# One-bank PSUM buffers for layer 1's transposes and last product, and no fetch of missing edges' rows in layer 2

## The chip, the cores and the metric

The kernel runs on one core of a Trainium2 chip. A core has four engines that compute and a set of DMA engines. TensorE (PE in the profile; PEld is its weight load) multiplies matrices and writes to PSUM, a memory of eight banks, each of which holds 512 float32 numbers in each of 128 partitions. VectorE (DVE) and ScalarE (ACT) work elementwise and read PSUM and SBUF. GpSimd (POOL) mostly issues gathers here, which are indirect DMAs with one row of a table for each partition. SyncE (SP) issues the plain DMAs. Each engine runs its own instructions in order and waits on semaphores for the others. The metric is the device time of one execution in microseconds, and the number given is a median over runs.

## What is computed

Two layers of graph attention over 10,000 nodes, each with a residual product, and a layer norm at the end. The edge list has 80,000 random edges in both directions and a self-loop for each node, 170,000 edges, sorted by destination. The reference adds the self-loops once more, so that each counts twice. Cut to what matters:

```python
def gat_conv(x, edge_index, W, a_src, a_dst, bias, heads, out_ch, concat):
    xl = (x @ W).reshape(n, heads, out_ch)
    alpha_src = jnp.einsum('nhc,hc->nh', xl, a_src)
    alpha_dst = jnp.einsum('nhc,hc->nh', xl, a_dst)
    e = leaky_relu(alpha_src[src] + alpha_dst[dst], 0.2)
    e = exp(e - segment_max(e, dst)[dst])
    alpha = e / (segment_sum(e, dst)[dst] + 1e-16)
    return segment_sum(xl[src] * alpha[:, :, None], dst) + bias

h = relu(layer_norm(gat_conv(x, ..., heads=4, out_ch=256, concat=True)))
h1 = h + (x @ Wr1 + br1)                                  # 10000 x 1024
h = layer_norm(gat_conv(h1, ..., heads=1, out_ch=768)) + (h1 @ Wr2 + br2)
out = layernorm(x + h)                                    # 10000 x 768, float32
```

## The kernel before

The work has three stages, and all three handle 79 tiles of 128 nodes.

**Preparation, with layer 1's first product (lines 602 to 670).** For each tile, x is multiplied by W1, and the product goes to `table1` in DRAM, with the logit terms of its four heads. A row has R1 = 1033 numbers: 1024 features, 4 + 4 logit terms, and minus the node's rank. Meanwhile the nodes are sorted by their number of edges, most first. Tile t in this order has `SLOTS[t]` edge slots for each node, a bound on the degrees that is known beforehand: 41 for the tile with the largest degrees, 8 for that with the smallest, 1377 in all. `slots` holds for each node and slot the row to be fetched. A node with fewer edges than its tile has slots has missing edges; their slot names row NP, one past the nodes' rows. That row is filled so that its logit is -1e30 and its weight zero.

**Layer 1 (`ordered_layer1`).** The tiles are taken in an order (`TURNS`) that runs from few slots up to 41 and down again. A ring of 29 row buffers in SBUF is filled by POOL, with one gather of 128 rows for each slot. `Ring.fetch` issues the gather of slot q + 29 when slot q has been used. The first 29 gathers read whatever their slot names. Later ones carry a bounds check at NP - 1, and a row past it is not fetched: the buffer keeps what it held. So that such a row has no weight, `logits` overwrites the logit columns of rows that it has read with -1e30 (line 489).

For each tile, DVE computes the logits, ACT their exp, and DVE the weights e. A few slots (`on_pe`, 1 to 4) are weighed on PE: ACT builds diagonal matrices of e, and PE multiplies the rows by them into the PSUM tile `acc`. ACT and DVE weigh the others (`multiply` at line 508, `weigh` at 515 and 519) and DVE adds them to `acc`. Then come the norm of the tile before (DVE, `h`), the transposes of x and h on PE, which ACT copies to SBUF (`columns`), x's product with Wr1 (`r`), and h's product with W2 (`to_layer2`), whose 770 columns ACT copies to `row` (`store`). They go to `table2`.

The order of the instructions is written by hand: the pools are under `manual_schedule`, and the loop over slots places the moves, the product for layer 2 and the next x's gather at given slots (`events`, `due`). PSUM is full: two `acc` tiles take four banks, `ps_h1` has one buffer of two banks for both transposes and the product for layer 2, and `ps_r1` has one of two banks for x's product.

**Layer 2 (`ordered_layer2`).** Again a ring, of 38 buffers with rows of R2 = 770 numbers from `table2`. A tile's first slot is its own nodes' rows, one contiguous block that SP loads (`ring.own`); POOL gathers the others, without a bounds check (line 453). `residual(t + 1)` multiplies h1 by Wr2 on PE, `weights_of(t + 1)` makes the weights and adds columns 512 to 767 of all slots on PE through diagonals (line 876), DVE weighs columns 0 to 511 (line 519), and `norms` finishes a tile over the next tile's slots and scatters it to the output (line 909).

Of the kernel before, what the change touches and what calls it, by code (L numbers as in the profile page):

```python
# [35 lines left out]
P = 128  # L36
# [43 lines left out]
def gnn_kernel(ctx, tc, x, x_cols, src, dst, src_col, dst_col, W1, a_src1, a_dst1, b1, g1, be1, Wr1, br1,  # L80
# [83 lines left out]
    def product(aT, w, n, pool=None):  # L164

        k = w.shape[1]
        p = (pool or ps_big).tile([P, 2 * BANK], F32, name="big")
        for c in range(0, n, BANK):
            e = min(n, c + BANK)
            for j in range(k):  # L170
                nc.tensor.matmul(p[:, c:e], aT[:, j, :], w[:, j, c:e], start=(j == 0), stop=(j == k - 1))  # L171
        return p
# [267 lines left out]
    class Ring:  # L440
# [8 lines left out]
        def fetch(self, upto):  # L449
            for q in range(self.issued, min(upto, TOTAL)):  # L450
                if q in self.own:
                    nc.sync.dma_start(self.slot(q), self.table[self.own[q] * P:(self.own[q] + 1) * P, :])
                elif q < self.size or self.own:
                    gather(self.slot(q), self.table[:, :], slots[:, q:q + 1])
                else:
                    gather(self.slot(q), self.table[:, :], slots[:, q:q + 1], bounds_check=NP - 1,
                           oob_is_err=False)
                self.issued = q + 1
# [12 lines left out]
    def logits(small, ring, lo, hi, ad, heads, c, top=None):  # L471


        n = hi - lo
        e = small.tile([P, ring.size, heads], F32, name="e")[:, :n]
        for a, b, rows in ring.parts(lo, hi):
            nc.vector.tensor_tensor(e[:, a - lo:b - lo], rows[:, :, c + heads:c + 2 * heads],
                                    ad[:, None, :].to_broadcast([P, b - a, heads]), op=OP.add)
        leaky(e, e)
        new = small.tile([P, heads], F32, name="new")  # L480
        nc.vector.reduce_max(new, e.rearrange("p k h -> p h k"), axis=AX.X)
        if top is not None:
            nc.vector.tensor_max(new, new, top)
        nc.vector.tensor_tensor(e, e, new[:, None, :].to_broadcast([P, n, heads]), op=OP.subtract)
        nc.scalar.activation(e, e, AF.Exp)
        for a, b, rows in ring.parts(lo, hi):
            if not ring.own:
                nc.vector.tensor_scalar(slots[:, a:b], rows[:, :, R1 - 1], -1.0, float(NP), op0=OP.mult, op1=OP.min)
                nc.vector.memset(rows[:, :, c + heads:], -BIG)
        return e, new  # L490

    def normalised(small, e, heads, t):
# [75 lines left out]
    def scaled(to, parts, mean_and_deviation, g, b):  # L568
# [6 lines left out]
            c = d  # L575
        nc.vector.reciprocal(inv, inv)
        nc.vector.scalar_tensor_tensor(to, to, inv, b, op0=OP.mult, op1=OP.add)

    def columns(to, a):

        p = ps_big.tile([P, 2 * BANK], F32, name="big").rearrange("p (k n) -> p k n", n=P)
        for i in range(to.shape[1]):
            nc.tensor.transpose(p[:, i, :], a[:, i * P:(i + 1) * P], ident)

        def move(j, e):
            return lambda: nc.scalar.copy(to[:, j:e, :], p[:, j:e, :])  # L586

        return [move(j, min(j + BANK // P, to.shape[1])) for j in range(0, to.shape[1], BANK // P)]

    def load(s, w):  # L590
        nc.sync.dma_start(s[:, :, :w.shape[1]], w.rearrange("(k p) n -> p k n", p=P))
# [84 lines left out]
        return order[:, TURNS[t]:TURNS[t] + 1]  # L676

    def ordered_layer1():
        nonlocal ps_big
        with tc.tile_pool(name="b1", bufs=1) as pool, tc.tile_pool(name="small1", bufs=2) as small, \  # L680
                tc.tile_pool(name="ps_acc1", bufs=2, space=PSUM) as ps_acc, \
                tc.tile_pool(name="ps_h1", bufs=1, space=PSUM) as ps_big, \
                tc.tile_pool(name="ps_r1", bufs=1, space=PSUM) as ps_r, tc.manual_schedule():
            ring = Ring(pool, table1, R1, RING1, {})
            ring.fetch(SLOTS[0])

            def fetch_x(t):
                xt = pool.tile([P, D0], F32, name="xt")
                gather(xt, x[:, :], nodes(t))
                return xt  # L690

            xt = fetch_x(0)
            ring.fetch(RING1)
# [40 lines left out]
            def store(t):  # L734

                nonlocal full
                row = pool.tile([P, R2], F32, name="row")
                nc.scalar.copy(row, full[:, :R2])
                full = None
                nc.sync.dma_start(table2[TURNS[t] * P:(TURNS[t] + 1) * P, :], row)  # L740

            for t in range(NT + 1):
                live, events = t < NT, []
                n = SLOTS[t] if live else 0
                first = done = on_pe(t) if live else 0
                whole = live and n <= ring.size
                if whole and not ready:
                    ahead = weights_of(t)
                    ready += itertools.islice(ahead, 2)

                def multiplied(upto):
                    nonlocal done
                    while whole and done < min(upto, n):
                        if shared(t, done):
                            multiply(ring.slot(FIRST[t] + done), e[:, done], DH1)
                        done += 1

                if whole:
                    e, acc = ready
                if last:  # L760
                    r, means = last
                    stats = deviation(small, pieces(means[:, :C1], BANK))
                for _ in ahead:
                    pass
                if full is not None:
                    store(t - 2)
                moves = []
                if live:
                    xT = pool.tile([P, K0, P], F32, name="xT")
                    moves = columns(xT, xt)  # L770
                    nc.sync.dma_start(x_d[t], xt)
                multiplied(first + 2)
                if last:
                    h = pool.tile([P, C1], F32, name="h")
                    scaled(h, [means[:, :C1]], stats, g1_b, be1_b)
                    nc.vector.scalar_tensor_tensor(h, h, 0.0, r[:, :C1], op0=OP.max, op1=OP.add)
                for move in moves:
                    move()
                multiplied(first + LEAD)
                if last:  # L780
                    hT = pool.tile([P, K1, P], F32, name="hT")
                    events = [(first + j, move) for j, move in enumerate(columns(hT, h))]
                if live:
                    r = product(xT, wr1, C1, ps_r)

                def to_layer2():
                    nonlocal full
                    nc.sync.dma_start(h1_d[t - 1], hT.rearrange("p k n -> p (k n)"))
                    full = product(hT, w2, R2)

                if last:
                    events.append((first + 2, to_layer2))

                def next_x():
                    nonlocal xt
                    xt = fetch_x(t + 1)

                if t + 1 < NT:
                    events.append((first + 2, next_x))

                def due(k):
                    while events and events[0][0] <= k:
                        events.pop(0)[1]()

                if live and not whole:
                    due(n)
                    acc = ps_acc.tile([P, 2 * BANK], F32, name="acc")
                    ad = small.tile([P, H1], F32, name="ad")
                    nc.vector.tensor_copy(ad, ring.slot(FIRST[t])[:, C1:C1 + H1])
                    attend_parts(small, ring, acc, acc, ad, None, H1, DH1, t)  # L810
                ready = []
                ahead = iter(())
                if whole and t + 1 < NT and SLOTS[t + 1] + LEAD <= ring.size:
                    ahead = weights_of(t + 1)
                for k in range(n if whole else 0):
                    multiplied(k + 1 + LEAD)
                    if n - LEAD <= k < n - LEAD + 2:
                        ready += itertools.islice(ahead, 1)
                    if k >= first:
                        weigh(acc, ring.slot(FIRST[t] + k), e[:, k], DH1, shared=shared(t, k))  # L820
                    ring.fetch(FIRST[t] + k + 1 + ring.size)
                    due(k)
                due(DEGREES)
                ready += itertools.islice(ahead, max(2 - len(ready), 0))
                last = None
                if live:
                    last = r, acc
# [405 lines left out]
```

## The time and the profile before

| what | value |
|---|---|
| median of 4 runs | 5651.07 us (5646.23 to 5659.61) |
| the profiled execution | 5652.43 us, span 5650.6 us |
| mean granted TensorE clock | 0.926 |
| PE busy | 4830.9 us (85%) |
| DVE busy | 4352.8 us (77%) |
| ACT busy | 3144.7 us (56%) |
| POOL busy | 3234.1 us (57%), of it 2654.1 us in 2675 ring gathers |
| DMA | 1591.38 MB, 282 GB/s on average |

The busy share of an engine is a mean over stages with different limits, so the prediction reads the profile by stage. A row of the groups has the line, the engine, the operation, what it writes and reads, how often, then busy us and mean ns. The row of a wait says which engine at which line waited for whom, with the total in us, how often, and the longest one. Gathers count as busy on POOL while POOL prepares them; the transfer itself runs later, on the DMA engines.

### The profile page before, as it was taken

What the parts mean: (1) busy time and instruction counts of PE and PEld (TensorE: products, weight loads), DVE (VectorE), ACT (ScalarE), POOL (GpSimd) and SP (SyncE); (2) the same over time, 40 slices, a digit from 0 to 9 for tenths busy, and PEclk for the clock granted to TensorE, in tenths of its full rate; (3) what the DMA queues carried; (4) which work ended last, traced back from release to release, by engine and by line L of the source; (5) the groups of instructions that cost most, each with busy time, mean ns of one, the idle gap of its engine ahead of it and who ended that gap; (6) DMA issues with size and microseconds to landing.
All of it is one profiled execution on the core that took longest, in us unless ns stands there. A gap on an engine that the chain in (4) does not pass through costs nothing. (4 is left out here: it accounts for less than half of the span.)

```text
span 5650.6 us, 59630 instructions
## 1 busy us (share of the span) xinstructions
PE 4830.9 (85%) x15008; PEld 2847.4 (50%) x15011; DVE 4352.8 (77%) x8008; ACT 3144.7 (56%) x8125; POOL 3234.1 (57%) x3159
## 2 busy tenths in 40 slices
PE   9999996999999874789999997988887737778898
PEld 3444443555555542455555554655555424555555
DVE  5883345999999888889999994977776666777788
ACT  3443344888888876889888872443333213333343
POOL 3447354555666655566665543666666665666663
PEclk9999998999999986899999998999898868888899
DMA  4333637899999986999999976998888878888885
GB/s 155 122 99 86 91 95 263 315 331 352 361 364 369 344 315 237 328 348 367 368 358 351 332 270 236 325 333 311 302 304 289 285 259 283 302 297 301 296 312 211
DMA packets 474308, 1591.38 MB, mean 282 GB/s; under 512 B 118327, under 2 KB 122487, under 8 KB 473958
## 3 DMA queue, kind: packets, MB, share of 16 engines
q0 software_dynamic: 322384, 1286.62, 64.2%
q1 hardware_dynamic: 149520, 297.43, 15.7%
q10 hardware_dynamic: 2054, 3.42, 0.2%
q8 instruction: 127, 2.08, 0.1%
q14 instruction: 223, 1.83, 0.1%
HBM read 1431.80 MB, written 177.29 MB: 285 GB/s over the span
## 5 line engine op out<-in xcount | busy, mean ns | idle before, releaser
L424 POOL DMA_INDIRECT ring<-table,slots x2675 | 2654.1, 992 | 1781.9 <-issue 618.5
L519 DVE SCALAR_TENSOR_TENSOR acc<-ring,e,acc 128x256 f32<-128x256 f32 (+1 forms) x2538 | 1571.3, 619 | 124.3 <-PE acc L719 44.6
L508 ACT ACTIVATE ring<-ring,e 128x256 f32<-128x256 f32 x3320 | 1351.8, 506 | 1.4 <-ACT ring L508 1.4
L515 DVE TENSOR_TENSOR acc<-acc,ring 128x1024 f32<-128x1024 f32 x830 | 1021.4, 1231 | 82.5 <-issue 9.0
L890 PE MATMUL big<-wr,w 128*128 128x512 f32 (+1 forms) x2528 | 909.9, 505 | 130.6 <-issue 128.8
L876 PE MATMUL big<-ring,diagonals 128*128 128x256 f32 x2672 | 703.7, 421 | 180.0 <-issue 135.0
L171 PE MATMUL big<-w,xT 128*128 128x512 f32 x1896 | 825.3, 597 | 24.5 <-DMA w<-in_W_dram 9.4
L171 PE MATMUL big<-wr,xT 128*128 128x512 f32 x1896 | 836.0, 597 | 9.0 <-issue 9.0
L171 PE MATMUL big<-w,hT 128*128 128x512 f32 (+1 forms) x2528 | 830.4, 486 | 1.2 <-ACT hT L586 1.2
L890 PEld LDWEIGHTS big<-wr,w 128*128 128x128 f32 x2528 | 497.9, 198 | 513.0 <-issue 480.3
L876 PEld LDWEIGHTS big<-ring,diagonals 128*128 128x128 f32 x2672 | 558.2, 212 | 327.1 <-issue 196.1
L171 PEld LDWEIGHTS big<-w,hT 128*128 128x128 f32 x2528 | 477.8, 189 | 374.0 <-issue 340.3
L875 ACT ACTIVATE diagonals<-ident,e 128x128 f32<-128x128 f32 x1336 | 407.6, 388 | 454.9 <-remote 164.1
L719 PE MATMUL acc<-ring,diagonals 128*128 128x256 f32 x1816 | 451.5, 406 | 226.3 <-ACT diagonals L713 186.2
L171 PEld LDWEIGHTS big<-w,xT 128*128 128x128 f32 x1896 | 361.7, 191 | 483.7 <-issue 465.2
L171 PEld LDWEIGHTS big<-wr,xT 128*128 128x128 f32 x1896 | 358.0, 192 | 430.5 <-issue 430.5
L719 PEld LDWEIGHTS acc<-ring,diagonals 128*128 128x128 f32 x1816 | 365.2, 204 | 305.4 <-ACT diagonals L713 201.4
L565 ACT ACTIVATE sd<-mv,eps 128x1 f32<-128x1 f32 x237 | 69.8, 295 | 612.8 <-DVE mv L563 349.4
L660 DVE TENSOR_TENSOR scr<-big,ad_b 128x1024 f32<-128x1024 f32 x79 | 96.7, 1224 | 377.8 <-ACT row L657 338.1
L713 ACT ACTIVATE diagonals<-ident,e 128x128 f32<-128x128 f32 x908 | 278.4, 387 | 118.3 <-DVE e L499 77.3
L665 POOL TENSOR_TENSOR row<-row,none 128x1024 f32<-128x1024 f32 x79 | 187.1, 2368 | 262.3 <-ACT row L657 260.0
L663 ACT ACTIVATE scr<-scr 128x256 f32<-128x256 f32 x632 | 253.5, 402 | 120.3 <-DVE scr L660 120.3
(172 smaller groups left out, 3768.7 us busy)
## 6 DMA issues: line engine op xcount, KB each, us to landing
ring<-table,slots POOLq DMA_INDIRECT x2675
table<-row SPq DMA_DIRECT2D x79, 516.0 KB
h_d<-hT SPq DMA_DIRECT2D x79, 512.0 KB
w<-h_d SPq DMA_DIRECT2D x79, 512.0 KB
table<-row SPq DMA_DIRECT2D x79, 385.0 KB
ring<-table SPq DMA_DIRECT2D x79, 385.0 KB
xT<-in_x_cols_dram SPq DMA_DIRECT2D x79, 384.0 KB
x_d<-xt SPq DMA_DIRECT2D x79, 384.0 KB
```

What stands on the lines that cost most here:

```text
L171: nc.tensor.matmul(p[:, c:e], aT[:, j, :], w[:, j, c:e], start=(j == 0), stop=(j == k - 1))
L424: nc.gpsimd.indirect_dma_start(out=to, out_offset=None, in_=table, in_offset=bass.IndirectOffsetOnAxis(ap=index, axis=0), **more)
L508: nc.scalar.activation(row[:, s], row[:, s], AF.Copy, scale=e[:, h:h + 1])
L515: nc.vector.tensor_add(acc[:, :c], acc[:, :c], row[:, :c])
L519: nc.vector.scalar_tensor_tensor(acc[:, s], row[:, s], e[:, h:h + 1], (acc if first is None else first)[:, s], op0=OP.mult, op1=OP.add)
L663: nc.scalar.activation(m[:, s], m[:, s], AF.Copy, accum_out=row[:, C1 + i * H1 + h:C1 + i * H1 + h + 1])
L665: nc.gpsimd.tensor_add(row[:, :C1], row[:, :C1], b1_b)
L713: nc.scalar.activation(diagonals[:, k * H1 + i, :], ident, AF.Copy, scale=e[:, k, i:i + 1])
L719: nc.tensor.matmul(acc[:, c:d], diagonals[:, k * H1 + i, :], ring.slot(FIRST[t] + k)[:, c:d], start=(k == 0 and c % BANK == 0), stop=(k == ...
L875: nc.scalar.activation(diagonals[:, k % G, :], ident, AF.Copy, scale=e[:, k, :])
L876: nc.tensor.matmul(to, diagonals[:, k % G, :], ring.slot(FIRST[t] + k)[:, ON_PE2:C2], start=False, stop=(k == n - 1), skip_group_check=True)
L890: nc.tensor.matmul(r[:, c:d], hT[:, j, :], wr2[:, j, c:d], start=False, stop=(j == K1 - 1 and (d < C2 or not whole(t))), skip_group_check= ...
```

## The change

**Layer 1.** The one two-bank buffer `ps_h1` becomes two buffers of one bank (`half`). `halves` transposes up to four blocks into a buffer and returns one ACT copy for each, where `columns` transposed all six or eight blocks into the two banks of one buffer. The product for layer 2 writes its columns 0 to 511 to one buffer and 512 to 769 to the other, and `store` copies them with two ACT instructions. x's gather for the first tile is issued ahead of all ring gathers, and this tile's transposes, copies and product with Wr1 are issued before the loop.

**Layer 2.** Gathers after the first 38 slots carry the bounds check, as layer 1's do, and `logits` overwrites the logit column of the rows it has read in layer 2 as well.

```diff
-                elif q < self.size or self.own:
+                elif q < self.size:
                     gather(self.slot(q), self.table[:, :], slots[:, q:q + 1])
                 else:
                     gather(self.slot(q), self.table[:, :], slots[:, q:q + 1], bounds_check=NP - 1,
...
             if not ring.own:
                 nc.vector.tensor_scalar(slots[:, a:b], rows[:, :, R1 - 1], -1.0, float(NP), op0=OP.mult, op1=OP.min)
-                nc.vector.memset(rows[:, :, c + heads:], -BIG)
+            nc.vector.memset(rows[:, :, c + heads:], -BIG)
...
-                tc.tile_pool(name="ps_h1", bufs=1, space=PSUM) as ps_big, \
+                tc.tile_pool(name="ps_h1", bufs=2, space=PSUM) as ps_half, \
                 tc.tile_pool(name="ps_r1", bufs=1, space=PSUM) as ps_r, tc.manual_schedule():
             ring = Ring(pool, table1, R1, RING1, {})
-            ring.fetch(SLOTS[0])
...
+            def halves(to, a):
+                moves, per = [], BANK // P
+                for j in range(0, to.shape[1], per):
+                    m = min(per, to.shape[1] - j)
+                    p = ps_half.tile([P, BANK], F32, name="half").rearrange("p (k n) -> p k n", n=P)
+                    for i in range(m):
+                        nc.tensor.transpose(p[:, i, :], a[:, (j + i) * P:(j + i + 1) * P], ident)
+                    moves.append(lambda j=j, m=m, p=p: nc.scalar.copy(to[:, j:j + m, :], p[:, :m, :]))
+                return moves
+
+            def from_x(t):
+                xT = pool.tile([P, K0, P], F32, name="xT")
+                moves = halves(xT, xt)
+                nc.sync.dma_start(x_d[t], xt)
+                return xT, moves
...
-                nc.scalar.copy(row, full[:, :R2])
+                for c, q in full:
+                    nc.scalar.copy(row[:, c:c + q.shape[1]], q)
...
+            xT, moves = from_x(0)
+            for move in moves:
+                move()
+            r = product(xT, wr1, C1, ps_r)
             for t in range(NT + 1):
...
-                if live:
-                    xT = pool.tile([P, K0, P], F32, name="xT")
-                    moves = columns(xT, xt)
-                    nc.sync.dma_start(x_d[t], xt)
+                if live and t:
+                    xT, moves = from_x(t)
...
-                    events = [(first + j, move) for j, move in enumerate(columns(hT, h))]
-                if live:
+                    events = [(first + j, move) for j, move in enumerate(halves(hT, h))]
+                if live and t:
                     r = product(xT, wr1, C1, ps_r)
...
-                    full = product(hT, w2, R2)
+                    full = []
+                    for c in range(0, R2, BANK):
+                        q = ps_half.tile([P, BANK], F32, name="half")[:, :min(BANK, R2 - c)]
+                        for j in range(K1):
+                            nc.tensor.matmul(q, hT[:, j, :], w2[:, j, c:c + q.shape[1]],
+                                             start=(j == 0), stop=(j == K1 - 1))
+                        full.append((c, q))
```

More of the change, by code (lines that the diff above doesn't have):

```diff
@@ L577, in scaled @@
         nc.vector.scalar_tensor_tensor(to, to, inv, b, op0=OP.mult, op1=OP.add)
[L579 to L588, printed above, removed]
     def load(s, w):
@@ L678, in ordered_layer1 @@
     def ordered_layer1():
-        nonlocal ps_big
         with tc.tile_pool(name="b1", bufs=1) as pool, tc.tile_pool(name="small1", bufs=2) as small, \
                 tc.tile_pool(name="ps_acc1", bufs=2, space=PSUM) as ps_acc, \
-                tc.tile_pool(name="ps_h1", bufs=1, space=PSUM) as ps_big, \
+                tc.tile_pool(name="ps_h1", bufs=2, space=PSUM) as ps_half, \
                 tc.tile_pool(name="ps_r1", bufs=1, space=PSUM) as ps_r, tc.manual_schedule():
             ring = Ring(pool, table1, R1, RING1, {})
-            ring.fetch(SLOTS[0])
             def fetch_x(t):
@@ L760, in ordered_layer1 @@
                 if last:
-                    r, means = last
+                    r_before, means = last
                     stats = deviation(small, pieces(means[:, :C1], BANK))
@@ L775, in ordered_layer1 @@
                     scaled(h, [means[:, :C1]], stats, g1_b, be1_b)
-                    nc.vector.scalar_tensor_tensor(h, h, 0.0, r[:, :C1], op0=OP.max, op1=OP.add)
+                    nc.vector.scalar_tensor_tensor(h, h, 0.0, r_before[:, :C1], op0=OP.max, op1=OP.add)
                 for move in moves:
```

## The prediction

> **What bounds the kernel now.** I cut the span by the stores: preparation to 885 us, layer 1 to 3445, layer 2 to the end at 5650. The table by stretches comes first (us, busy us of each engine with its instructions, TensorE clock, DMA share, GB/s).
>
> ```profile
> 1140.00:1400.00 260.00, 249.56 (x839) 148.42 (x838) 240.40 (x408) 210.50 (x503) 150.87 (x150) 0.99 0.95 341
> 1400.00:1820.00 420.00, 394.71 (x1354) 237.90 (x1353) 384.51 (x622) 366.47 (x903) 270.10 (x262) 1.00 0.98 363
> ...
> 3720.00:4460.00 740.00, 610.79 (x1970) 400.14 (x1969) 542.23 (x1102) 256.09 (x623) 471.21 (x487) 0.89 0.87 304
> ```
>
> Layer 1 is level: PE 96%, DVE 92%, DMA 95 to 98%. In layer 2 none stands out; POOL seems lowest at 64%, but that leaves out what lies between its gathers. Next, the waits of PE and of DVE over 1000 to 3440 us (total, times, longest):
>
> ```profile
> PE acc L719 <- ACT diagonals L713: 185.7, 32, 60.5
> PE big L583 <- ACT xT L586: 64.3, 62, 1.3
> ...
> DVE acc L519 <- PE acc L719: 34.4, 39, 3.3
> DVE e L477 <- DMA ring<-table,slots: 25.1, 10, 5.9
> ```
>
> PE's first wait belongs mostly to the 41-slot tile (129.6 of it from 2000 to 2400). The second is the change's target, about 1 us a tile. DVE hardly waits at all. The timeline of one tile shows the target wait:
>
> ```profile
> 1523.05 0.82 PE L583 MATMUL big<-ident,xt 128*128 128x128 f32 x6
> ...
> 1523.96 0.86 ACT L586 COPY xT<-big 128x512 f32<-128x512 f32 x2 [0.20 <-issue]
> ...
> 1524.88 0.33 PE L583 MATMUL big<-ident,h 128*128 128x128 f32 x1 [1.01 <-ACT xT L586]
> ```
>
> h's transposes need the one buffer, so both copies of xT must end first. Last, the gathers at line 424, layer 2 first, then layer 1 (min/median/max ns):
>
> ```profile
> L424 POOLq EVENT_SEMAPHORE  x1330: 17/43/13351, 3500.0 to 5579.0; - x190
> L424 POOL DMA_INDIRECT ring<-table,slots x1264: 940/946/1729, 3500.2 to 5582.8; - x181
> ...
> L424 POOL DMA_INDIRECT ring<-table,slots x1315: 984/989/2012, 1001.3 to 3360.8; - x188
> ...
> L424 POOLq MOVE  x1313: 29/29/29, 1002.0 to 3357.9; - x188
> ```
>
> Layer 1's gathers carry a bounds check, layer 2's do not: 989 against 946 ns, and one MOVE more. By start times, 1010 of layer 2's 1263 steps from gather to gather are back to back at a median of 1.251 us; layer 1's back-to-back steps lie at 1.295 or 1.337. So layer 2's POOL is really taken for 1.25 us x (n - 1) + 1.3 (the output's scatter): 22.6 of a 27 to 28 us tile of 18 slots. PE needs about 21 there (residual 11.6, bias 0.7, 18 x 0.47), DMA 24 (17 x 64 packets x 0.279 us / 16, and 4.8 for the rest). POOL is the fullest part of layer 2 by a little, and logits start 5 to 10 us after a tile's last gather was issued in the tiles 22 to 54 in turn.
>
> **Layer 1's buffers.** The spacing of line 788's stores has plateaus: 25.13, 26.87, 28.60, 30.33 us, steps of 1.73 = 4 matmuls of 0.43, one more slot on PE each. Those are PE's: its busy time plus the 1.0 us wait. I count 27 of 78 intervals on a plateau. With halves, the first four transposes of h wait for the first xT copy alone. In the timeline above ACT is free at 1523.76, the copy takes 0.58, so h's transposes start near 1524.40, not 1524.88; the second copy (0.38) ends within the first four transposes (4 x 0.11). Gain: 0.5 us per plateau interval. But DVE is next: its busy time and its own 35 to 104 ns gaps leave 0 to 0.8 us in most of these intervals (none at 28.60, 2.0 in three of 25.13). The smaller of 0.5 and this slack, summed, is 9 us. The other 51 intervals are held by DVE, by DMA (0.98), or near the 41-slot tile by rows; I give them nothing. The product for layer 2 only writes its two banks to two tiles: the same matmuls, hidden under nothing new. The store becomes two copies, 0.58 + 0.38 by the xT copies against 0.78: +0.15 us of ACT, beside PE's diagonals, and ACT is at 81 to 90%. Uncovered that is 79 x 0.15 = 12 us of loss, the pessimistic end; I take 0.
>
> **The start of layer 1.** x's gather moves ahead of all ring gathers (POOL, one 1.25 us step later for the first rows, which already waited for x's landing: nothing), its x_d store moves ahead on SP (idle then), and the transposes, copies and 24 matmuls of tile 0 go before tile 0's weights. Now:
>
> ```profile
> 910.27 0.92 PE L583 MATMUL big<-ident,xt 128*128 128x128 f32 x6
> ...
> 919.58 0.86 ACT L586 COPY xT<-big 128x512 f32<-128x512 f32 x2 [10.59 <-remote]
> ...
> 920.22 1.22 PE L171 MATMUL big<-wr,xT 128*128 128x512 f32 x1 [9.03 <-issue]
> ```
>
> The product runs 920.2 to 932.6. Moved, x lands near 893; if the unexplained 9 us stall comes along, the product ends at 917, tile 0's diagonals queue behind it (917 to 920 instead of 907 to 910), and tile 1 begins about 3 us earlier than at 934.4; without the stall it is 8. Behind the moved copies ACT's exp for tile 0 waits, which is not due before 904.7. If the stall is longer it costs up to 5. I take -4.
>
> **Layer 2's missing rows.** Counting the graph that the reference draws, 6,256 of 1377 x 128 slot rows are missing, 5,212 of them after the first 38 slots; 27 gathers would be wholly empty. The skip works in layer 1: its 4,132-byte packets number 171,044 = 176,256 - 5,212. In layer 2 those rows are 16.1 MB; by the packet records an empty slot's packets (all reading one row) take 356 ns on average against 279. The DMA queues rarely stand behind: a gather's last packet ends 4.4 us after its issue, through most of the stage. So what a skip can save is the tail, about 64 x 356 / 16 = 1.4 us when a tile's last gather is empty: 10 such tiles lie where rows are awaited, 5 more are half empty, and the 41-slot tile has 12. At 1.2 us, 0.6 us and 3 us in all, weighted 0.75 as below: -14.
>
> The price is on POOL: 1,264 gathers, +43 ns (989 - 946), and at the steps +44 to +86. I take 55. In the 45 tiles 10 to 54 (857 gathers) I count three quarters: all of it if POOL's chain of gathers sets the period, half if the ring's loop does (a slot is refilled two tiles later, so two periods share one run of gathers). 857 x 0.055 x 0.75 = 35. The other 407, in tiles where logits start 11 to 22 us after the last issue or PE is full, at a fifth: 4.5. Sum +40. An empty gather is no cheaper to issue: layer 1's 27 empty ones also took 989. The added memset (62 to 158 ns in layer 1, 1 or 2 a tile) lies on DVE while exp runs; queued behind it are weighings of the tile before. Hidden; 79 x 0.16 = 13 us if not.
>
> [...]
>
> **Sum.** -9 - 4 - 14 + 40 = +13. The profiled execution took 5652.4 (span 5650.6), 1.4 above the median of 5651.1; against the median I expect 5664.
>
> **Rivals.** *The wait absorbs it (faster).* POOL waits 195.7 us for PE's line 876 and 92.3 for an unnamed release between 3600 and 5600. If slots come free by PE's pace, longer issues only eat this wait. Then layer 2 pays at most 10 and keeps 14 to 25 of lighter DMA, layer 1 gives 13 to 25: about 5625. For it: PE straggles through residual products, at 0.89 of its clock. It decides where POOL's wait per tile exceeds 18 x 0.055 = 1 us and rows are not awaited. Against: 80% of steps are back to back, and there is no gap between two tiles' batches.
> *Half price (no change).* The ring's loop halves both price and tail; layer 1 gains its 9 to 15: 5645 to 5661.
> *Full price (slower yet).* +86 ns on all 857 is 74, and TensorE's clock falls with longer idling (0.99 where PE is full, 0.84 at 4620 to 5060): about 5700.
> *The skip does not happen*, because slots do not hold the past-the-end number in layer 2: layer 1 wrote them, so 1 in 50; then only the price is left, 5678.
>
> **How the numbers follow.** The forecast with the full price has 0.44 (0.08 of it near 5700), no change 0.28, faster 0.28. Changes under 0.2% (11 us) can hardly be told from none here. The forecast's own range is 5655 to 5690; to hold 8 in 10 with the faster case: 5628 to 5702.
>
> **What would show it.** Right: layer 2's gathers at 989 to 996 ns with a MOVE each, bytes down by 16 MB, layer 2 longer by 20 to 40 us; PE's wait for the xT copies down from 64 to 30 us or less, plateaus shorter by up to 0.5; layer 1 shorter by about 13. Wrong: layer 2 not longer although gathers are at 989 (absorbed), its POOL wait for PE down by some 60 us; or plateaus down by a whole microsecond, so that DVE had slack that I did not see.

## The result and the profile after

| | median | runs | ratio to the kernel before |
|---|---|---|---|
| kernel before | 5653.57 us (5639.26 to 5671.98) | 55 | |
| changed kernel | 5636.04 us (5619.47 to 5659.88) | 34 | 0.9973 (0.9966 to 0.9980) |

The change makes this kernel 0.27% faster by the ratio; the medians lie 17.5 us apart. I had forecast 5664, slower. The profiled execution of the changed kernel took 5659.84 us, 24 above its median: it shows the parts, but its layer 2 is a long one.

The stretches of before, in the changed kernel (us, busy us and instructions of PE, PEld, DVE, ACT and POOL, TensorE clock, DMA share, GB/s):

```profile
1140.00:1400.00 260.00, 250.34 (x846) 149.90 (x845) 241.60 (x411) 211.96 (x517) 152.85 (x152) 0.99 0.95 342
1400.00:1820.00 420.00, 396.28 (x1352) 237.46 (x1351) 385.47 (x625) 367.74 (x920) 269.69 (x262) 1.00 0.99 365
3720.00:4460.00 740.00, 610.27 (x1949) 401.38 (x1947) 534.12 (x1122) 255.78 (x622) 480.51 (x476) 0.88 0.86 295
```

Layer 1 is as level as before. In layer 2 POOL is busier (480.5 against 471.2 us) with fewer instructions, and PE as busy as before. The waits of PE and DVE over 1000 to 3440 us (total, times, longest):

```profile
PE acc L725 <- ACT diagonals L719: 196.2, 31, 60.0
PE half L687 <- ACT xT L688: 24.8, 39, 1.0
PE half L687 <- issue: 20.7, 15, 13.5
...
DVE e L477 <- DMA ring<-table,slots: 29.5, 15, 4.3
DVE acc L519 <- PE acc L725: 28.5, 30, 3.3
```

The target wait, 64.3 us before, is 24.8; PE's other waits at that line grew, from 36 us in all to 51. In the timeline of one tile, h's transposes start 0.51 us after x's end, where they had waited 1.01:

```profile
1521.44 0.82 PE L687 MATMUL half<-ident,xt 128*128 128x128 f32 x6
...
1522.13 0.86 ACT L688 COPY xT<-half 128x512 f32<-128x512 f32 x2
...
1522.77 1.09 PE L687 MATMUL half<-ident,h 128*128 128x128 f32 x8 [0.51 <-issue]
```

And layer 2's gathers, with the MOVE and the price (min/median/max ns):

```profile
L424 POOL DMA_INDIRECT ring<-table,slots x1261: 992/998/1782, 3499.6 to 5591.3; - x181
L424 POOLq MOVE  x1259: 10/29/725, 3500.0 to 5587.7; - x180
```

946 has become 998 ns, and the pitch of gathers that follow each other went from 1.251 to 1.303 us. The bytes fell from 1591.38 to 1575.43 MB, the 16 MB of the forecast. So the shorter wait, the dearer gather and the lighter traffic are all there at about their sizes, and yet the time went the other way.

### The profile page after: what moved, and what is told of

Same layout as the page of the kernel before. It is cut to its first block, busy times and chain, and to the rows that moved or that the text cites. A ratio compares the mean times of both kernels' runs of the same rounds, so it can differ in the third digit from the quotient of the medians.

```text
span 5658.0 us, 61010 instructions
## 1 busy us (share of the span) xinstructions
PE 4855.9 (86%) x15008; PEld 2862.1 (51%) x15011; DVE 4353.4 (77%) x8124; ACT 3147.6 (56%) x8204; POOL 3294.6 (58%) x3159
## 2 busy tenths in 40 slices
DMA packets 474319, 1575.43 MB, mean 278 GB/s; under 512 B 120928, under 2 KB 125088, under 8 KB 473958
## 5 line engine op out<-in xcount | busy, mean ns | idle before, releaser
L424 POOL DMA_INDIRECT ring<-table,slots x2675 | 2715.5, 1015 | 1705.8 <-issue 621.3
L892 PE MATMUL big<-ring,diagonals 128*128 128x256 f32 x2672 | 724.8, 431 | 155.4 <-issue 85.5
L803 PE MATMUL half<-w,hT 128*128 128x512 f32 (+1 forms) x2528 | 830.4, 486 | 0.0
L892 PEld LDWEIGHTS big<-ring,diagonals 128*128 128x128 f32 x2672 | 573.9, 218 | 309.7 <-issue 151.9
L803 PEld LDWEIGHTS half<-w,hT 128*128 128x128 f32 x2528 | 477.8, 189 | 372.8 <-issue 333.2
```

The costliest lines, as they stand in the source:

```text
L424: nc.gpsimd.indirect_dma_start(out=to, out_offset=None, in_=table, in_offset=bass.IndirectOffsetOnAxis(ap=index, axis=0), **more)
L803: nc.tensor.matmul(q, hT[:, j, :], w2[:, j, c:c + q.shape[1]], start=(j == 0), stop=(j == K1 - 1))
L892: nc.tensor.matmul(to, diagonals[:, k % G, :], ring.slot(FIRST[t] + k)[:, ON_PE2:C2], start=False, stop=(k == n - 1), skip_group_check=True)
```

## The experiments

Each group of runs shared a chip with runs of the kernel before, and that kernel's own median differs between groups: 5653.57 (I call this chip A), 5623.22 and 5624.89 (B), and 5398.03, 5399.55, 5397.53 (C). B and C are kinds of chip: the two groups on B ran on chips numbered 6 and 7, the three on C on chips 12, 3 and 1. Layer 1 takes the same on all within 0.6%; layer 2 is 200 us shorter on C. Ratios are to the kernel before on the same chip; sizes in us are differences of medians, each first reduced by the kernel before on its own chip where groups are crossed.

**Theories.** *A, absorbed*: POOL's dearer gathers eat its own waiting. *B, all of it is layer 1*: price and skip cancel. *C, the prediction's terms.* Theories D to H are told where they come up; the letters of theories and of chips have nothing to do with each other.

### First group, chip B

**e1, layer 1 alone.** The changed kernel, with

```diff
-                elif q < self.size:
+                elif q < self.size or self.own:
...
-            nc.vector.memset(rows[:, :, c + heads:], -BIG)
+                nc.vector.memset(rows[:, :, c + heads:], -BIG)
```

> The changed kernel with layer 2 as it was before (no bounds check in its gathers, no extra memset): the layer 1 part alone. Theory A, 'absorbed' (layer 2's dearer gathers eat POOL's own waiting, and the skip brings 10 to 25 us): layer 1 is worth the 7 us that the one profile shows, so about 5646, a ratio of 0.9988 to the kernel before, and the changed kernel is faster than this one by some 10 us. Theory B, 'all of it is layer 1' (price and skip of layer 2 cancel): about 5636, ratio 0.997. Theory C, the prediction's own terms (layer 1 -13, layer 2 a loss of 26): 5640, and the changed kernel slower than it.

Measured 5614.71 us, 0.9988 (0.9977 to 0.9998): 8.5 us, about half of the result on A, if layer 1 gains the same there.

**e2, layer 2 alone.** The kernel before, with the two edits of e1 the other way round.

> The kernel before with layer 2's skip alone (bounds check and memset in layer 2; layer 1 as before). Theory A, 'absorbed': 10 us faster than before, about 5643, ratio 0.998, while POOL's gathers take 998 ns instead of 946 and its wait for PE shrinks by about the 60 us that it is busier. Theory B, 'all of it is layer 1': 5653, ratio 1.000. Theory C, the prediction's terms (+40 price, -14 skip): 5679, ratio 1.0046.

Measured 5596.40 us, 0.9962 (0.9945 to 0.9979): layer 2's part gains 27 us, more than any theory had.

**e3, the price without the skip.** The changed kernel, with

```diff
-                    gather(self.slot(q), self.table[:, :], slots[:, q:q + 1], bounds_check=NP - 1,
+                    gather(self.slot(q), self.table[:, :], slots[:, q:q + 1],
+                           bounds_check=NP if self.own else NP - 1,
                            oob_is_err=False)
```

> The changed kernel, but layer 2's bound is one row higher, so that the index of a missing edge is inside it: every gather pays the bounded issue, and nothing is skipped (the 16 MB are moved as before). Its distance to the run with layer 1 alone is the price by itself (and the memset); its distance to the changed kernel is what the skip is worth. Theory A, 'absorbed': price 10 us or less, skip 15 to 25: about 5650 to 5656, ratio 0.9995 to 1.0005. Theory B, 'price and skip cancel at some size': 5636 plus the size, 5650 to 5675. Theory C, the prediction's terms: +40 over layer 1 alone, 5680, ratio 1.005.

Measured 5588.68 us, 0.9943 (0.9928 to 0.9958). All theories miss. Nothing is skipped, every gather is 52 ns dearer, and it is 26 us faster than layer 1 alone. If e2's 27 us and layer 1's 8.5 add up, the whole change would stand at 5588, just here: then on this chip the skip is worth about nothing, and the price is a gain. The whole change itself was never run on B.

**e4, the skip at an eighth of the price.** The changed kernel, with

```diff
-                elif q < self.size:
+                elif q < self.size or (self.own and not may_miss(q)):
```

where `may_miss` holds for the last two slots of a tile and the last 14 of the 41-slot tile.

> The changed kernel, but in layer 2 only the last two slots of each tile and the last fourteen of the 41-slot tile carry the bounds check: 164 gathers after the first filling, which hold all 5,212 missing rows; the other 1,100 are issued as before. The skip is whole, the price is an eighth (164 x 52 ns = 9 us of POOL's time). Theory A, 'absorbed': like the changed kernel, 5630 to 5636 (ratio 0.996 to 0.997). Theory B or C, 'the price is on the path': faster than the changed kernel by what the price was, 20 to 40 us: 5596 to 5616 (ratio 0.990 to 0.9935).

Measured 5625.48 us, 1.0012 (1.0000 to 1.0024), 11 us slower than layer 1 alone. Skip and memset are kept, the price is nearly gone, and so is the gain. No theory had this; why the kernel falls behind layer 1 alone is not shown.

### Second group, chip C

**e5, the changed kernel again.**

> The changed kernel itself, to stand beside the other three on one chip. The four runs so far leave a puzzle: the dearer gathers without any skip gained 26 us over layer 1 alone. Theory D, 'pace': in layer 2 a slower chain of gathers is itself the gain, and the skip is worth about nothing: like the price without the skip, ratio 0.9945. Theory E, 'the skip costs': rows that are not fetched lose what the price gains (the changed kernel stood at 0.9973 in its own comparison): ratio 0.997, 10 to 15 us slower than the price alone.

Measured 5405.82 us, 1.0015 (1.0007 to 1.0024): slower here. The sign of the change differs between chips A and C.

**e6, the price alone.** e3's bound, and the memset only in layer 1.

> As the price without the skip (layer 2's bound one row higher, nothing skipped), and layer 2's extra memset is left out too: the bounded issue by itself on top of layer 1 alone. Theory D, 'pace': the gain is the issue's, so it stays: ratio 0.994 or a little less. Theory F, 'the memset does it' (it delays DVE and ACT by a little at each tile): the gain goes, ratio 0.9988 or the 1.000 to 1.005 that the prediction's price would give.

Measured 5420.06 us, 1.0042 (1.0030 to 1.0054). What gained 26 us on B (there with the memset) costs about 30 here.

**e7, another delay.** e1, with

```diff
+                elif self.own and q >= self.size:
+                    nc.gpsimd.memset(pace, 0.0)          # pace: one element
+                    gather(self.slot(q), self.table[:, :], slots[:, q:q + 1])
```

> Layer 1 alone (layer 2's gathers plain, no memset), but ahead of every gather of layer 2 after the first filling POOL writes one element of a scratch tile: another delay in the place of the bounded issue, some 50 to 150 ns by the trace's smallest instructions. Theory D, 'pace': any delay of about that size gains, ratio 0.993 to 0.996; if the delay comes out at twice the 52 ns or more, the gain shrinks or turns. Theory G, 'it is the form of the gather, not the delay': no gain, ratio 0.999 or a loss of up to 60 us (1.01).

Measured 5398.76 us, 1.0002 (0.9993 to 1.0010). The write took 89 ns but fell into the 0.30 us between two gathers: their pitch stayed at 1.254 us. So it was no test of the pace.

**e8, the memset alone.** e1 with the memset in both layers.

> Layer 1 alone with layer 2's extra memset, its gathers plain (all fetched). Theory D, 'pace': the memset is not the gain: ratio 0.9988 to 1.001 (0 to 13 us lost against layer 1 alone). Theory F, 'the memset does it': ratio 0.994.

Measured 5388.67 us, 0.9981 (0.9973 to 0.9990): no loss against layer 1 alone (0.9983, below). The memset is hidden.

### What the two chips do differently

Here is one residual product (36 records, the same instructions in every tile) on B, in e1:

```profile
5097.68 1.02 PE L903 MATMUL big<-w,ident 128*128 128x512 f32 x2
5098.54 7.03 PE L906 MATMUL big<-wr,w 128*128 128x512 f32 x16
5105.41 0.59 PE L903 MATMUL big<-w,ident 128*128 128x256 f32 x2
5105.84 2.54 PE L906 MATMUL big<-wr,w 128*128 128x256 f32 x11
5109.19 0.38 PE L906 MATMUL big<-wr,w 128*128 128x256 f32 x1 [0.82 <-issue]
5111.99 0.38 PE L906 MATMUL big<-wr,w 128*128 128x256 f32 x1 [2.42 <-issue]
5113.39 0.59 PE L906 MATMUL big<-wr,w 128*128 128x256 f32 x1 [1.02 <-issue]
5114.79 1.01 PE L906 MATMUL big<-wr,w 128*128 128x256 f32 x2 [0.81 <-issue]
```

and on C, in layer 1 alone (g3 below):

```profile
4837.18 1.02 PE L903 MATMUL big<-w,ident 128*128 128x512 f32 x2
4838.04 7.03 PE L906 MATMUL big<-wr,w 128*128 128x512 f32 x16
4844.90 0.59 PE L903 MATMUL big<-w,ident 128*128 128x256 f32 x2
4845.34 3.62 PE L906 MATMUL big<-wr,w 128*128 128x256 f32 x16
```

11.8 us on C, 18.1 on B, and nothing in the trace releases the stops: they are "issue", time in which PE waits for nothing that the profile shows. The starts after them lie 2.80, 1.40 and 1.40 us apart, multiples of 0.70, as at 77 of the 100 stops of over 0.3 us in this run's line 906. Half clock (a granted clock of 0.5) adds to the stops: in before, the slow products exceed 11.77 us by 191 us in all, of which 125 are stops, and 21 of the 25 spend over 1 us at half clock. From each run's records I counted, for layer 2, which of the 79 residual products take more than 15 us, and added up PE's work in stretches at half its clock (3520 to 5360 us) and the time from the first gather to the last output's scatter:

| run | chip | slow residual products | PE at half clock, us | layer 2, us |
|---|---|---|---|---|
| before | A | 25 | 280 | 2188 |
| changed (the long execution) | A | 28 | 339 | 2202 |
| e1 layer 1 alone | B | 21 | 303 | 2150 |
| e3 price, no skip | B | 16 | 252 | 2133 |
| e2 layer 2 alone | B | 14 | 260 | 2118 |
| g3 layer 1 alone | C | 0 | 153 | 1938 |
| g2 price alone | C | 0 | 165 | 1963 |
| g1 changed | C | 0 | 161 | 1953 |

The waits say who is last ("remote" is a wait whose releaser the profile does not find). PE and DVE over 3500 to 5300 us in e1, chip B:

```profile
PE big L906 <- issue: 113.2, 105, 2.4
PE big L892 <- issue: 104.6, 72, 23.3
...
DVE e L477 <- DMA ring<-table,slots: 125.1, 27, 10.4
DVE st L561 <- remote: 88.3, 14, 11.4
DVE sd L576 <- ACT sd L565: 63.3, 10, 8.5
DVE st L561 <- PE big L906: 36.8, 5, 12.8
```

and in g3, chip C:

```profile
PE big L892 <- ACT diagonals L891: 181.1, 35, 22.9
...
DVE e L477 <- DMA ring<-table,slots: 162.5, 43, 9.9
...
DVE st L561 <- PE big L892: 3.3, 5, 0.8
```

Line 561 is the norm's statistics. The instruction that waits here, also in the "remote" rows, reads PE's part of the sum (`big`) and waits for the same semaphore, which PE's matmuls raise. So on B DVE stands 125 us for PE there, as long as for rows; on C it stands 3 for PE, and 162 for rows. This points to PE, or its signals, on B, and to POOL's chain of gathers on C.

Whether it is PE's work or its signals on A and B, the traces leave open. By their ends of matmuls, which are modelled, DVE's statistics start more than 2 us after the last matmul into their tile in 27 of 39 such waits in before and in 26 of 40 in e1, but in none of 5 in g3 (from 3520 us on). PE's updates of the semaphore come in bursts there: from 3520 to 5300 us, 407 of the 1210 recorded in before and 408 of 1238 in e1 lie within 0.1 us of the one ahead, none of 1787 in g3. So PE computes later than its records say, or its signals come late. The traces of A and B also lack records (1210 updates for 1532 matmuls that raise the semaphore in before, 1787 for 1788 in g3), so "issue" and "remote" say less there; whether the recording itself plays a part was not tested.

### Third group, chip B: PE relieved and loaded

**f1 and f2.** e1 and e6, with half of the residual's matmuls left out:

```diff
-                    for j in range(K1):
+                    for j in range(K1 // 2):
```

> Layer 1 alone (layer 2's gathers plain), and in layer 2 TensorE is relieved: the residual product takes 4 of its 8 column blocks, so 16 of its 32 matmuls with the weights are left out (some 5.4 us of PE a tile). To be read against the next run, which differs by the bounded issue alone. By itself it shows where PE binds layer 2: if it binds (the chips where the kernel before takes 5620 to 5650 us), it is 50 to 150 us faster than before; if POOL binds (the chip with 5400), 10 to 40 us.

> The same relieved kernel with the bounded issue in every gather of layer 2 (its bound holds the index of missing edges, so nothing is skipped; no memset). Theory H, 'PE's slow stretches hide the price': with PE relieved POOL's chain is the bound on any chip, and the price shows: 25 to 40 us slower than the run before it, a ratio higher by 0.005 to 0.007. Theory D, 'a slower pace is itself a gain on these chips': it stays 20 us or more faster than the run before it wherever the kernel before takes 5620 or more.

Measured 5528.68 and 5538.33 us, 0.9830 (0.9809 to 0.9850) and 0.9848 (0.9828 to 0.9868). That PE binds on B is shown: half of its residual work gone gives 88 us over layer 1 alone. The price changes sign, from -26 to +10, but is less than the 25 expected; nearly a third of the shortened products are still slow (25 and 22 of 79 at over 1.25 times their median).

**f3 and f4.** e1 and e6, with

```diff
+                    for j in range(K1 // 2):
+                        nc.tensor.matmul(r[:, c:d], hT[:, j, :], wr2[:, j, c:d], start=(j == 0), stop=False,
+                                         skip_group_check=True)
                     nc.tensor.matmul(r[:, c:d], ident, xt[:, c:d], start=True, stop=False,
```

> Layer 1 alone (gathers plain), and in layer 2 TensorE is loaded: half of the residual product (16 matmuls, some 5.4 us of PE a tile) is done once more ahead of it and overwritten. To be read against the next run. By itself: PE needs 27 us of a tile's 24 to 28, so 100 to 400 us slower than before.

> The same loaded kernel with the bounded issue in every gather of layer 2, nothing skipped, no memset. Theory H, 'PE hides the price': with PE as the bound POOL's longer issues fall into its waiting: within 10 us of the run before it (ratio the same within 0.002), on any chip. The prediction's own step (three quarters of 55 ns on the path, whatever PE does): 25 to 40 us slower. Theory D, 'pace': 20 us or more faster.

Measured 5827.59 and 5772.06 us, 1.0357 (1.0334 to 1.0379) and 1.0260 (1.0240 to 1.0281). With PE loaded the dearer gather gains 55.5 us. Absorption alone (theory H) would give 0, so it falls as a full account; the dearer gathers change what PE does. The groups of PE's instructions in f3 and then f4, over 3500 to 5700 us (count, busy us, mean ns, idle before), show where:

```profile
L909 PE MATMUL big<-wr,w 128*128 128x256 f32 x1183 | 319.1, 417 | 87.2 <-issue 86.9
L904 PE MATMUL big<-wr,w 128*128 128x512 f32 x592 | 274.3, 604 | 32.9 <-DVE w L519 24.6 <-issue 8.2
```

```profile
L909 PE MATMUL big<-wr,w 128*128 128x256 f32 x1216 | 312.7, 402 | 56.6 <-issue 55.8
L904 PE MATMUL big<-wr,w 128*128 128x512 f32 x609 | 281.9, 603 | 33.4 <-DVE w L519 25.8 <-issue 7.3
```

The unexplained stops within the product's last 16 records fall from 87 to 56 us. All 79 residual products, first to last matmul, add up to 1539 us in f3 and 1487 in f4; these 52 us match the 51 by which layer 2 is shorter in the two profiles (2359 and 2308).

### Fourth and fifth group, both chip C

**g1, g2, g3.** Changed kernel, price alone (e6) and layer 1 alone (e1), once more, together.

> The changed kernel, beside its own parts on one chip. If the kernel before takes about 5620 or more (PE with slow stretches): theory H+D, 'on such a chip the dearer gather costs nothing or gains, the skip is worth 15 us at most either way': ratio 0.994 to 0.9975. If it takes about 5400: the prediction's terms, 1.0015 as before.

> Bounded issue in all of layer 2's gathers, nothing skipped, no memset; layer 1 as changed. Slower chip: 15 to 30 us faster than layer 1 alone, ratio 0.994 to 0.996. Faster chip: 1.004, some 30 us slower than layer 1 alone.

> Layer 1 alone, layer 2 as before: the reference of the other three. 0.9988 on the slower chip (as measured before); 0.998 to 0.999 on the faster one, since layer 1 takes the same time on both.

Measured 5405.95 us, 1.0014 (1.0005 to 1.0023); 5418.07 us, 1.0035 (1.0021 to 1.0049); 5391.23 us, 0.9983 (0.9974 to 0.9992). On one chip: layer 1 -8.3 us, price +26.8, skip with its memset -12.1, sum +6.4. The first two repeat the second group's numbers.

**g4 and h1, longer delays.** e7, with `pace` of 64 and of 128 elements.

> Layer 1 alone with plain gathers, and POOL writes 64 elements of a scratch tile ahead of each gather of layer 2. The write of one element (89 ns) fell wholly into the 0.30 us that lie between two gathers: their pitch stayed at 1.254 us. This one should lengthen it by 40 to 130 ns, like the bounded issue's 52 or up to twice that. Slower chip: 'pace' says 10 us or more faster than layer 1 alone; 'form of the gather' says no faster than it. Faster chip: slower than layer 1 alone by three quarters of the added pitch times 857, 25 to 85 us.

> Layer 1 alone with plain gathers, and POOL writes 128 elements of a scratch tile ahead of each gather of layer 2: pitch 1.29 to 1.31 us in place of 1.254. Slower chip: 'pace' says like the bounded issue, ratio 0.994 to 0.996; 'form of the gather' says 0.9988 or more, as layer 1 alone or slower. Faster chip: 'price is time on POOL, whatever it is spent on' says like the bounded issue, 1.003 to 1.005, 20 to 35 us over layer 1 alone.

g4: 5399.48 us, 1.0002 (0.9993 to 1.0011). Its write of 141 ns was still hidden, with a pitch of 1.257 us. As with e7, 8 to 9 us over layer 1 alone are not explained by the pitch. h1: 5431.78 us, 1.0066 (1.0052 to 1.0079). Its write showed at last:

```profile
4150.66 0.19 POOL L455 MEMSET pace<- 1x128 f32 x1
4151.01 0.95 POOL L425 DMA_INDIRECT ring<-table,slots  x1 [0.16 <-issue]
4151.97 0.19 POOL L455 MEMSET pace<- 1x128 f32 x1
4152.32 0.95 POOL L425 DMA_INDIRECT ring<-table,slots  x1 [0.16 <-PE big L896]
```

From start to start it is 1.31 us, at the median 1.305. On C that costs 43 us over layer 1 alone, more than the 20 to 35 expected, or 34 without the 8 that the hidden writes cost as well.

**h2, the price alone, beside h1.**

> The bounded issue beside it (nothing skipped, no memset). Slower chip: 0.994 to 0.996. Faster chip: 1.0035 to 1.0042 as before.

Measured 5415.57 us, 1.0036 (1.0022 to 1.0049), 26 us over layer 1 alone, at a pitch of 1.303. So on C a longer pitch costs time without a skip and without the bounded form. The same pitch cost 17 us more with the writes than with the bound; 8 of these also appear with hidden writes, and the rest is open. Whether on B the gain too comes from the pace and not from the form stays open: none of the delayed runs (e7, g4, h1) fell on that kind of chip.

No version won everywhere. Layer 1 alone is the one kernel that was faster than before on both B (0.9988) and C (0.9983); the fastest on B was e3.

## Why the prediction was wrong, point by point

- **Layer 1's buffers (-9).** Right in mechanism and nearly in size. The wait fell to 24.8 us (30 forecast), the plateaus of 25.13 and 26.87 us lie at 24.64 and 26.37, that of 28.60 at 28.3 to 28.4. From the first h store to the last, 2488.6 us became 2481.9 in the profile, and 2476 to 2484 in the other runs with the new buffers. ACT's longer store (0.93 us a tile in place of 0.78) was hidden, as taken.
- **The start (-4).** Nothing. From POOL's first gather of layer 1 to the first h store it is 60.7 us before and 60.6 after. The product is done by 907, so the 9 us stall did not come along, but then DVE starts tile 0's weighing late:

```profile
908.91 0.22 DVE L499 TENSOR_TENSOR e<-e,total 128x32 f32<-128x32 f32 x1
...
909.62 1.99 PE L725 MATMUL acc<-ring,diagonals 128*128 128x256 f32 x8 [2.28 <-issue]
...
926.05 2.06 DVE L519 SCALAR_TENSOR_TENSOR acc<-ring,e,acc 128x256 f32<-128x256 f32 x4 [16.92 <-issue]
```

  The weighing waits for DVE's own and PE's semaphores, and PE's last matmul into `acc` ends at 911.61 by the trace, 14.4 us earlier. On C (e5) the same kernel has no such delay, and there first gather to first h store takes 58.9:

```profile
909.64 2.56 PE L725 MATMUL acc<-ring,diagonals 128*128 128x256 f32 x8 [3.07 <-ACT diagonals L719]
...
912.24 2.06 DVE L519 SCALAR_TENSOR_TENSOR acc<-ring,e,acc 128x256 f32<-128x256 f32 x4 [3.09 <-PE acc L725]
```

- **The skip (-14).** On chip C it is worth 12.1 us (g2 to g1) and 14.2 (e6 to e5), both with the memset, which is hidden as taken. On B, crossed from e1, e2 and e3, it is worth about nothing; that a tile there does not end with its rows would explain it, but is not shown.
- **The price (+40).** On C it is 26 to 30 us (g2, h2, e6). The gather grew by 52 ns, as taken (55), but 1,264 x 0.052 = 66 us of POOL's time became 26 to 30 on the path, four tenths, where I had three quarters over the middle tiles and a fifth elsewhere. On B it is -26. The sign named for absorption came only in part on A: POOL's wait for PE's line 876 (now 892), 195.7 us, fell to 174.5, not by some 60.
- **The sum (+13).** On C it is +6.4 and +7.8: the forecast's sum with the terms of layer 1 and the price smaller. On A, where the result was taken, it is -17.5; there no part was run by itself. If layer 1 gives its 8.5 there as on B, layer 2 gives the other 9.

The step that failed is the one that made POOL the bound: "PE needs about 21 there (residual 11.6, ...)", against 22.6 of POOL. 11.6 is about the time of a residual product that runs freely (11.77). In the trace of before, 25 of 79 are slow, and the mean of all 79 is 1140.5 / 79 = 14.4 us. With that mean PE needs about 24, more than POOL. By the prediction's own figures DMA, with 24, already stood above POOL, and none of the three came to the tile's 27 to 28 us; that difference should have been looked for. The waits of DVE in layer 2 of before (3500 to 5560 us), which I did not read, point the same way:

```profile
DVE st L561 <- remote: 144.2, 20, 11.7
DVE e L477 <- DMA ring<-table,slots: 102.4, 20, 12.2
DVE sd L576 <- ACT sd L565: 89.0, 11, 11.9
DVE st L561 <- PE big L890: 25.9, 4, 9.6
```

DVE stood 170 us for the part of the sum that PE makes, and 102 for rows. So on A, too, layer 2 hung more on PE's results than on POOL's gathers. That this is why the price was no loss there is inferred from B; on A it was not tested. My count of back-to-back gathers (80% of the steps) decided nothing: it is 81% on B, where POOL is not the bound (1017 of 1260 in e1), and 86% on C, where it is (1077 of 1259 in g3).

The rival that came nearest is the first, "the wait absorbs it", with its own argument, that PE straggles through residual products; even it had no gain from the price, which on B is there and stays unexplained. It had 0.28 and the forecast 0.44, and what decided between them was 21 against 22.6 us.

## What to carry to other kernels

Take what an engine needs for a tile from the mean over its tiles in the trace, not from the shortest case: here 11.8 or 14.4 us for one product decided which engine counted as the bound, and with it the forecast's sign. Where no engine's sum reaches the period, look for the rest first. To see who is the bound, read whom the finishing engine waits for (here DVE's wait at the norm's statistics), rather than how densely the suspected one works. And a change of a few tenths of a per cent can change sign from chip to chip (here 0.9973 on A and 1.0015 on C), so its parts are best compared on one.

## What the runs showed of the hardware

- The same program's layer 2 took 1938 us on one chip and 2150 on another (layer 1 alone, g3 and e1), while layer 1 was the same within 0.3% (2478.9 and 2483.9 us between its first and last h store). On the longer one PE stops within residual products, 102 times for over 0.3 us in e1. 72 of these stops lie in a product's last 16 records, which read the same `hT` as its first 16, and at 77 of the 100 at line 906 the start after the stop lies a multiple of 0.70 us after the one ahead. The instruction queues end a fetch in the last 1 us of only 3 of the 102. What makes the stops is open.
- On the chips with the stops, DVE starts later than PE's records would let it: by the trace's modelled ends, 27 of 39 waits in layer 2 of before (A) and 26 of 40 in e1 (B) ended over 2 us after the last matmul into the tile, and up to 17 us after it in before; on C (g3) none of 5 did. In the changed kernel the weighing of tile 0 started 14.4 us after its last matmul on A, and 0.04 us after it on C (e5).
- On B, dearer gathers went with shorter residual products: with 52 ns more on each gather the kernel with a loaded PE gained 55.5 us (f3 to f4), its 79 residual products took 1487 us in all in place of 1539, and 15 of them took over 1.25 times the median, in place of 22. Why is open.
- In layer 2 of before (3520 to 5360 us) TensorE's granted clock was 0.5 in 50 stretches, each a multiple of 3.41 us long (3.41 to 64.85). In the 3.41 us ahead of them PE was busy for 0.27 of the time on average, for less than half in 47 of the 50, and for 0.57 at the most; in the last 3.41 us of a stretch it was busy for 0.97 on average. 280 us of PE's records in layer 2 ran in such stretches.
- On C, a write of 89 or 141 ns on POOL between two gathers hardly lengthened their pitch (1.254 us in e7 and 1.257 in g4, 1.251 without in g3), and one of 194 did (1.305 in h1).
